# A 3x3 convolution on group-normalised images: some images by four result columns at a time, F(4,3), in pairs, the others plainly

## The chip, the cores and the metric

The kernel runs on one core of a Trainium2 chip. A core has TensorE (PE), which multiplies a 128x128 block of weights with a stream of columns into PSUM; VectorE (DVE), ScalarE (ACT) and GpSimd (POOL), which work on 128 partitions element by element; and DMA queues, of which SyncE (SP) and GpSimd issue those used here. The metric is the device time of one execution in microseconds (us), the median of several runs.

## The reference

The input holds 160 images of 128 channels and 32x32 points in float32. Each image is normalised over groups of four channels, without learned scale. The weights are five sets of 128x128x3x3 numbers, quantised in two steps from their common range. Image `i` of each five is convolved (3x3, padding 1) with set `i`, and the input is added to the result.

```python
    beta = jnp.max(U); alpha = jnp.min(U)
    s1 = (beta - alpha) / 3.0
    v1 = s1 * floor(U / s1)
    s2 = s1 / 5.0
    v2 = s2 * floor((U - v1) / s2)
    w = (v1 + v2).reshape(128 * 5, 128, 3, 3)
    act = conv(gn(x).reshape(32, 5 * 128, 32, 32), w, padding=1, groups=5)
    return x + act.reshape(x.shape)
```

## The kernel before, in words

Channels lie on the 128 partitions, and an image is a row of 1,024 float32 numbers per partition. The kernel handles the images of set 0 first, then set 1, and so on, so that "image 0 to 159" below is that order; two images make a chunk, which is loaded by one DMA. The instructions are written in the order in which each engine runs them (a manual schedule), so an engine's program order is the order of the Python calls.

Precision: a normalised image is split into a high part and a low part, both float16, and both are multiplied with the float16 integer weights.

One image goes through these steps:

- **Statistics** (`measure`, L241 and L248): two passes of ScalarE, over the sum and over the squares, far ahead of use. Means and variances of the channel groups come from small matmuls (`means`, `variances`), and small operations of VectorE, ScalarE and GpSimd make the reciprocal deviation from them (`deviations_by_vector`, `deviation`, `power`, `scales_by_vector`).
- **Combinations.** From image 7 on there are two kinds. A *combined* image uses F(2,3) across columns: for each pair of neighbouring result columns, four combinations of four input columns replace six products by four. `outer_columns` (L678) and one subtraction (L708) on GpSimd and `combine` (L690, L697) on VectorE make a float32 tile `v` of 2,048 columns; `high_combined` (ScalarE, L738) takes its high part and `low_combined` (VectorE, L744) its low part. A *row* image is normalised on GpSimd (L714), its high part (L648) is used as it stands, and only its low part (L751) is combined, over pairs of rows (`combinations`, L764 to L773). `combined()` says which kind an image is: every second up to 30, then three of five, and from image 130 three of four.
- **Products** (`product` L843, `taps` L788): a combined image takes 24 matmuls (four combinations, three rows of taps, two parts) of 512 or 496 columns, a row image 18 for the high part and 12 for the low part. The two middle combinations go to the banks `m1` and `m2_ps` one image ahead (`sums_of_pairs`). ScalarE takes `m2_ps` out (`leave`, L891), VectorE writes half the sum and half the difference into the two result banks (`pairs`, L903 and L905), and the other products add to them.
- **Result.** ScalarE copies the banks to SBUF (L929), and a DMA of GpSimd's queue adds them in DRAM to the image, which SP's queue had stored there before (L953, `store_input` L968). The first three and the last four images are added by VectorE instead (L946, L936).

The weights of the next set are quantised meanwhile on VectorE and ScalarE in small steps (`Later`, `make_column`), put between the other operations. GpSimd's operations on images are tied by `after` to an operation of VectorE, so that they run beside `pairs`. Images are loaded again into a buffer (of eleven) when its images have been combined or normalised.

Of the kernel before, what the change touches and what calls it, by code (L numbers as in the profile page):

```python
# [8 lines left out]
F32 = mybir.dt.float32  # L9
I32 = mybir.dt.int32  # L10
MM = mybir.dt.float16
# [11 lines left out]
LAST = 4  # L23
# [3 lines left out]
LIFT = 2.0**14  # L27
# [3 lines left out]
WIDEST = 40.0  # L31
# [5 lines left out]
class Later:  # L37


    def __init__(self, steps=(), pace=0.0):  # L40
        self.steps = iter(steps)
        self.pace, self.due = pace, 0.0
        self.scalar = False

    def next_image(self):
        self.due += self.pace

    def take(self, count, last=None):
        for _ in range(count):
            if not self.scalar and self.due >= 1.0:  # L50
                step = next(self.steps, None)
                self.scalar = step is SCALAR
                if not self.scalar:
                    last = step or last
                    self.due -= 1.0
        return last

    def take_scalar(self):
        if self.scalar:
            next(self.steps)  # L60
            self.scalar = False

    def finish(self):
        run(self.steps)
# [141 lines left out]
class Statistics:  # L206
# [5 lines left out]
    def __init__(self, nc, small, gavg, mhalf, nb, scale, name):  # L212
        self.nc, self.small, self.gavg, self.mhalf = nc, small, gavg, mhalf
        self.nb, self.scale, self.name = nb, scale, name
        self.late = self.shifted = False
# [74 lines left out]
    def deviations_by_vector(self):  # L290
# [3 lines left out]
        self.ngm, self.twice, self.dv = (self.tile(tag, [self.nb]) for tag in ("ngm", "twice", "dv"))  # L294
        means = self.pg[:, 0, :]
        vector.tensor_scalar_mul(self.twice, means, 2.0)
# [7 lines left out]
    def scales_by_vector(self):  # L304

        vector = self.nc.vector
        vector.tensor_scalar_mul(self.rstd, self.rstd, self.scale)
        if self.shifted:
            self.shift = self.tile("shift", [self.nb])
            vector.tensor_tensor(self.shift, self.ngm, self.rstd, ALU.mult)  # L310

    def scales(self):
# [5 lines left out]
        self.twice = self.tile("twice", [self.nb])  # L318
        nc.gpsimd.tensor_scalar_mul(self.twice, self.ngm, 2.0)
# [66 lines left out]
class Main:  # L386
# [24 lines left out]
    STAT_LEAD = 15  # L411
    FURTHER = 11
    LOAD_LEAD = 18
    CHUNKS = 11
    STEADY = 7
    BY_VECTOR = (8, 10, 11, 14, 19, 24, 29, 34)
    FIFTHS = 30
    THIRDS = 130
    EARLY = 8
    FIRST = 3  # L420
    HURRIED = (0, 2, 4, 8, 24)
# [6 lines left out]
    def __init__(self, tc, ctx, keep, x, u, out):  # L428
# [20 lines left out]
        self.rows = pool("rows", 5)  # L449
        self.wide = pool("wide", 2)  # L450
        self.wide_parts = pool("wide_parts", 4)
        self.evac = pool("evac", 2)
        self.sums = pool("sums", 3)
        self.unread = pool("unread", 1)
        self.small = pool("small", 3)
        self.ps_eo = pool("ps_eo", 2, space=PSUM)
# [8 lines left out]
        self.pair = [self.m1a, self.m2_ps]  # L465

# [4 lines left out]
        self.tables, self.wts, self.across = {}, {}, {}  # L471
        self.columns = []

        cuts = [0, 2, 4, 8, 12, 16, 20, *range(24, self.imgs + 1, 8)]
# [88 lines left out]
    def keep_taps(self, n, col):  # L563

        P = self.P
        if n not in self.tables:
            self.tables[n] = self.wpool.tile([P, ROW, 5, P], MM, tag="wt", name=f"wt{n}")
# [9 lines left out]
    def sums_across(self, n, engine):  # L577

        across = self.across[n] = self.wpool.tile(
            [self.P, 2, ROW, self.P], MM, tag="across", name=f"across{n}"  # L580
        )
        yield from self.both_sums(
            engine, across[:, 0], across[:, 1], *(self.tables[n][:, c, self.G] for c in range(ROW))
        )

    def sums_of_set(self, n):

        wt = self.tables[n]
        yield from self.both_sums(
            self.nc.vector, wt[:, :, self.SUM], wt[:, :, self.DIFF],  # L590
            *(wt[:, :, k] for k in range(ROW)),
        )
        yield from self.sums_across(n, self.nc.vector)
# [15 lines left out]
    def stats_of(self, k):  # L609
        if k not in self.stats:  # L610
# [5 lines left out]
            self.stats[k].shifted = not self.combined(self.groups[k].start)  # L616
# [699 lines left out]
```

## Time and profile before

| what | value |
|---|---|
| median of 3 runs | 967.3 us (965.7 to 967.39) |
| the profiled execution, its own time | 964.56 us |
| its span on the core | 962.5 us |
| TensorE busy | 927.8 us |
| VectorE busy | 902.6 us |
| ScalarE busy | 862.7 us |
| GpSimd busy | 460.1 us |
| moved by DMA | 254.22 MB, mean 264 GB/s |
| granted TensorE clock, mean | 0.995 |

The busy time of an engine is the union of its instructions' spans. Neighbouring instructions of VectorE and of ScalarE overlap by some hundredths of a microsecond, and matmuls by more, so a row's mean time for one is longer than the distance at which they follow each other. A row of the table of groups reads: line, engine, operation, output <- inputs, shapes, count | busy us, mean ns of one | idle us of the engine just before, and what ended it.

### The profile page before, as it was taken

What the parts mean: (1) busy time and instruction counts of PE and PEld (TensorE: products, weight loads), DVE (VectorE), ACT (ScalarE), POOL (GpSimd) and SP (SyncE); (2) the same over time, 40 slices, a digit from 0 to 9 for tenths busy, and PEclk for the clock granted to TensorE, in tenths of its full rate; (3) what the DMA queues carried; (4) which work ended last, traced back from release to release, by engine and by line L of the source; (5) the groups of instructions that cost most, each with busy time, mean ns of one, the idle gap of its engine ahead of it and who ended that gap; (6) DMA issues with size and microseconds to landing.
All of it is one profiled execution on the core that took longest, in us unless ns stands there. A gap on an engine that the chain in (4) does not pass through costs nothing.

```text
span 962.5 us, 13034 instructions
## 1 busy us (share of the span) xinstructions
PE 927.8 (96%) x4432; PEld 433.8 (45%) x4432; DVE 902.6 (94%) x1269; ACT 862.7 (90%) x1167; POOL 460.1 (48%) x477
## 2 busy tenths in 40 slices
PE   2899989999999999999999999999999999999997
PEld 1344434444444444444444444444444444444443
DVE  7989999999899999989999999899999998999993
ACT  5879989999899999999999999999999999997660
POOL 4344434456445445554545445545444366565640
PEclk9999999999999999999999999999999999999999
DMA  9079999999999999999999999999999999856563
GB/s 349 36 267 345 334 348 320 325 321 325 328 321 323 317 295 308 272 306 254 295 251 289 284 293 297 282 277 286 267 273 267 282 279 269 172 91 107 91 107 112
DMA packets 67450, 254.22 MB, mean 264 GB/s; under 512 B 5296, under 2 KB 5296, under 8 KB 67376
## 3 DMA queue, kind: packets, MB, share of 16 engines
q1 hardware_dynamic: 45344, 173.09, 48.0%
q0 software_dynamic: 22032, 80.23, 44.4%
q8 instruction: 36, 0.59, 0.2%
q14 instruction: 38, 0.31, 0.1%
HBM read 89.19 MB, written 164.10 MB: 263 GB/s over the span
## 4 chain that ended last, share of the span: by engine, by line


## 5 line engine op out<-in xcount | busy, mean ns | idle before, releaser
L788 PE MATMUL eo<-hi,wt 128*128 128x496 f16 (+3 forms) x1170 | 310.8, 376 | 2.4 <-DVE eo L905 1.7
L843 PEld LDWEIGHTS <-wt 128*128 128x128 f16 x1884 | 183.9, 99 | 211.5 <-DVE eo L905 2.7
L744 DVE SCALAR_TENSOR_TENSOR vl<-v,rstd,vh 128x2048 f16<-128x2048 f32 x94 | 221.8, 2360 | 0.2 <-ACT vh L738 0.2
L843 PE MATMUL eo<-vh,wt 128*128 128x512 f16 x561 | 210.1, 375 | 1.2 <-DVE eo L905 1.2
L843 PE MATMUL eo<-vl,wt 128*128 128x512 f16 x561 | 210.1, 374 | 0.0
L738 ACT ACTIVATE vh<-v,rstd 128x2048 f16<-128x2048 f32 x94 | 188.2, 2002 | 4.8 <-DVE v L697 4.3
L929 ACT COPY sum<-eo 128x1024 f32<-128x1024 f32 x153 | 161.0, 1052 | 32.3 <-PE eo L843 31.7
L788 PEld LDWEIGHTS <-wt 128*128 128x128 f16 x1242 | 121.2, 99 | 142.8 <-DVE eo L905 4.9
L678 POOL TENSOR_SCALAR v<-xt,ngm 128x64 f32<-128x64 f32 x94 | 79.1, 842 | 202.0 <-DVE vl L744 86.9
L248 ACT ACTIVATE junk<-xt,mv 128x1024 uint8<-128x1024 f32 x152 | 174.4, 1148 | 0.3
L241 ACT ACTIVATE junk<-xt 128x1024 uint8<-128x1024 f32 x152 | 160.5, 1056 | 13.3 <-DMA xt<-in_x_dram 10.0
L714 POOL TENSOR_SCALAR z<-xt,ngm,rstd 128x1024 f32<-128x1024 f32 x49 | 93.3, 1904 | 165.1 <-DVE rows L773 55.0
L843 PEld LDWEIGHTS <-across 128*128 128x128 f16 x1128 | 110.8, 98 | 131.9 <-issue 4.9
L843 PE MATMUL eo<-rows,wt 128*128 128x512 f16 x378 | 143.5, 380 | 0.0
L953 POOL DMA_DIRECT2D out_dram<-sum x153 | 133.7, 874 | 14.4 <-ACT sum L929 6.6
L690 DVE TENSOR_TENSOR v<-xt 128x960 f32<-128x960 f32 x94 | 114.0, 1212 | 0.0
L843 PE MATMUL m<-vl,across 128*128 128x496 f16 (+1 forms) x282 | 106.4, 377 | 2.1 <-DVE vl L744 2.1
L891 ACT ACTIVATE m<-m 128x512 f32<-128x512 f32 x157 | 93.7, 597 | 14.1 <-PE m L843 13.7
L843 PE MATMUL m<-vh,across 128*128 128x496 f16 (+1 forms) x282 | 106.2, 376 | 0.2 <-ACT m L891 0.2
L708 POOL TENSOR_TENSOR v<-xt 128x512 f32<-128x512 f32 x94 | 97.2, 1034 | 0.0
L751 DVE TENSOR_TENSOR lo<-z,hi 128x1024 f16<-128x1024 f32 x66 | 80.6, 1221 | 0.0
L286 POOL TENSOR_TENSOR rstd<-ve,mhalf 128x8 f32<-128x8 f32 (+2 forms) x24 | 42.3, 1761 | 65.1 <-DVE rows L773 21.1
(150 smaller groups left out, 1166.3 us busy)
## 6 DMA issues: line engine op xcount, KB each, us to landing
xt<-in_x_dram SPq DMA_DIRECT2D x78, 1024.0 KB, 9.6
out_dram<-sum POOLq DMA_DIRECT2D x153, 512.0 KB, 8.7
out_dram<-xt SPq DMA_DIRECT2D x76, 1024.0 KB, 14.2
out_dram<-xt SPq DMA_DIRECT2D x7, 512.0 KB, 3.3
u<-in_L_conv_U_dram SPq DMA_DIRECT2D x4, 576.0 KB, 13.6
xt<-in_x_dram SPq DMA_DIRECT2D x4, 512.0 KB, 10.1
range<-in_L_conv_U_dram SPq DMA_DIRECT2D x3, 576.0 KB, 8.3
u<-in_L_conv_U_dram SPq DMA_DIRECT2D x2, 288.0 KB, 3.1
```

The lines of the kernel that those rows point to most:

```text
L241: self.nc.scalar.activation(junk, image, ACTF.Copy, scale=-1.0 / image.shape[1], accum_out=self.mv[:, j, 0:1],)
L248: self.nc.scalar.activation(junk, image, ACTF.Square, bias=self.mv[:, j, 0:1], accum_out=self.mv[:, j, 1:2],)
L690: nc.vector.tensor_tensor(self.view(v, 1, (511, 2), (half, H), (1, half - 1)), self.view(x, 1, (1, 2), (W, H), (2, half - 1)), self.view(x ...
L708: ins = nc.gpsimd.tensor_sub(self.v[i][:, 1536:], odd, even)
L714: ins = nc.gpsimd.tensor_scalar(z, self.image(i), st.ngm[:, j], st.rstd[:, j], ALU.add, ALU.mult)
L738: self.nc.scalar.mul(vh, self.v[i], st.rstd[:, j])
L744: yield self.nc.vector.scalar_tensor_tensor(vl, self.v[i], st.rstd[:, j], self.hi[i], ALU.mult, ALU.subtract)
L788: nc.tensor.matmul(self.bank(target, a)[:, first:end, c0:c1], self.wts[n, col][:, k, :], tile[:, s0 : s0 + 2 * (end - first) - 1 : 2, c0 + ...
L843: self.nc.tensor.matmul(out, weights, moving, start=start and j == 0, stop=False, skip_group_check=True)
L891: self.nc.scalar.mul(m2, self.m2_ps, 0.5)
L929: nc.scalar.copy(self.as_banks(i, self.sum[i]), self.flat(i, eo))
L953: added = self.nc.gpsimd.dma_start(self.ov[n, :, b], self.sum.pop(i), accum_op=ALU.add)
```

## The change

Two kinds of images remain after image 4. **Quad** chunks (43 of the 80, list `QUADS`; 86 images) use F(4,3) across columns: four neighbouring result columns come from six combinations of six input columns, for both images of the chunk at once. The other 69 images are **plain**: both parts go through all nine taps as they stand, 36 matmuls of up to 512 columns. A quad image takes 36 matmuls of 256 or 248 columns (six combinations, three rows of taps, two parts).

- On GpSimd, `differences` makes the difference of the left and right neighbours of every point (960 points by one subtraction, and the two edge columns by two operations of 32 points each). `combine`'s share of GpSimd and the normalising there are gone.
- On VectorE, `inner_points` and `outer_points` make the six combinations of a chunk from the image and from the differences. They read every fourth number of a row (`every_fourth`, a step of 16 bytes). `low_quad` takes the low part (1,536 columns per image), `high_quad` on ScalarE the high part. `combinations`, `pairs` and the row kind are gone but for images 3 and 4.
- The four inner products of an image go to `m1` and `m2_ps`, two to a bank. `leave` takes `m2_ps` out; `sum_and_difference` (four operations on PSUM for a chunk) and `four_points` (four on SBUF) make the four result columns' share. Two columns are started in the result banks, where the two outer products are added (`quad_main`), and two are written to every fourth place of `quad_sum`; `quad_result` copies the other two beside them, and one DMA adds both images in DRAM.
- Plain images are normalised and split on ScalarE, their low part is made on VectorE (1,024 columns), and their banks are copied out by ScalarE as before.
- The loop runs over **units**: one quad chunk with one plain image (23 units) or two (20 units), after nine single images and before the last two, which are plain. `unit` writes each engine's order: TensorE does the inner products of the chunk, the first plain image, the outer products and, if there is one, the second plain image.
- Statistics are made in groups of five images rather than eight, eight image buffers replace eleven, the tables of a set hold five combinations of the three columns of taps, and four images rather than eight are measured on VectorE.

```diff
-    BY_VECTOR = (8, 10, 11, 14, 19, 24, 29, 34)
+    CHUNKS = 8
+    BY_VECTOR = (8, 10, 11, 14)
+    QUADS = (5, 7, 9, 11, 13, *(c for c in range(15, 64) if c * 7 % 12 < 7), *(c for c in range(64, 79) if c % 3))
...
+    def differences(self, i):
...
+        return [
+            pool.tensor_scalar(d[:, :, 0:1], x[:, :, 1:2], st.ngm[:, k], 1.0, ALU.add, ALU.mult),
+            pool.tensor_scalar(
+                d[:, :, W - 1 :], x[:, :, W - 2 : W - 1], st.ngm[:, k], -1.0, ALU.add, ALU.mult
+            ),
+            pool.tensor_sub(d[:, :, 1 : W - 1], x[:, :, 2:], x[:, :, : W - 2]),
+        ]
+    def every_fourth(self, t, start, count=1):
+        return self.view(t, start, *([(1, count)] if count > 1 else []), (4, 512))
+    def inner_points(self, c):
+        u = self.u[c] = self.wide.tile([self.P, 6, NB, 256], F32, tag="u", name=f"wide{c}")
+        vector = self.nc.vector
+        x = self.chunks[c]
+        ab = u[:, 3:6:2].rearrange("p k j q -> p k (j q)")
+        vector.scalar_tensor_tensor(
+            ab, self.every_fourth(x, 0, 2), -4.0, self.every_fourth(x, 2, 2), ALU.mult, ALU.add
+        )
+        for j in range(NB):
+            st, k = self.column_of(c * NB + j)
+            vector.scalar_tensor_tensor(
+                u[:, 2, j], u[:, 5, j], st.six[:, k], u[:, 3, j], ALU.add, ALU.add
+            )
+        vector.tensor_sub(u[:, 4], u[:, 5], u[:, 3])
+    def outer_points(self, c):
+        u, d, vector = self.u[c], self.d.pop(c), self.nc.vector
+        flat = u.rearrange("p k j q -> p k (j q)")
+        vector.scalar_tensor_tensor(
+            flat[:, 0:2], self.every_fourth(d, 2, 2), 0.25, self.every_fourth(d, 0, 2),
+            ALU.mult, ALU.subtract,
+        )
+        for slot, by in ((3, 2.0), (5, -2.0)):
+            vector.scalar_tensor_tensor(
+                flat[:, slot], self.every_fourth(d, 1), by, self.every_fourth(d, 2),
+                ALU.mult, ALU.add,
+            )
...
+    def quad_product(self, target, i, slot, start):
+        n, _ = self.place(i)
+        eighth = self.W // 4
+        for step in self.KS:
+            shift = (step - 1) * eighth
+            first, end = max(0, -shift), 256 - max(0, shift)
+            for j, source in enumerate((self.hi[i], self.v[i])):
+                self.nc.tensor.matmul(
+                    target[:, first:end],
+                    self.quads[n][:, slot - 1, step] if slot else self.wts[n, 0][:, step],
+                    source[:, slot, first + shift : end + shift],
...
+    def sum_and_difference(self, i):
...
+        for k, op in enumerate((ALU.add, ALU.subtract)):
+            self.nc.vector.scalar_tensor_tensor(
+                self.sd[c][:, k, :, j], m13, THIRDS, m24, ALU.mult, op
+            )
+    def four_points(self, c):
...
+        vector.tensor_add(flat[:, 0], sd[:, 0, 0], sd[:, 0, 1])
+        vector.scalar_tensor_tensor(flat[:, 1], sd[:, 1, 1], 8.0, sd[:, 1, 0], ALU.mult, ALU.add)
+        for k, by, s in ((1, 2.0, 1), (2, 4.0, 0)):
+            vector.scalar_tensor_tensor(
+                self.every_fourth(total, k), sd[:, s, 1], by, sd[:, s, 0], ALU.mult, ALU.add
+            )
...
+    def unit(self, u):
...
+        for j in range(NB):
+            if coming is not None:
+                self.high_quad(coming * NB + j)
+            for which in (1, 0):
+                self.sum_of_pairs(c * NB + j, which)
+            self.leave(c * NB + j)
+        self.left_over()
+        take(1)
+        for j in range(NB):
+            if wide is not None:
+                before = self.last_but_one()
+                for ins in self.differences(wide * NB + j):
+                    self.after(ins, before)
+            self.sum_and_difference(c * NB + j)
...
+        if mine:
+            self.main(mine[0], 0, first_place)
...
+        self.four_points(c)
...
+                self.low_quad(coming * NB + j)
...
+            self.main(mine[0], 1)
...
+        self.quad_main(c, second_place)
...
+            self.inner_points(wide)
...
+            self.outer_points(wide)
...
+            self.low_part(prepared[0])
+        if len(mine) > 1:
+            self.quad_result(c)
...
+            self.main(mine[1], 0, self.columns_on_the_way)
...
+            self.main(mine[1], 1)
```

## The prediction

> **What bounds the kernel now.** First I read the busy table and the stretches. The lines give the length of the stretch, then for each engine its busy time, then TensorE's granted clock, the DMA engines' share and GB/s.
>
> ```profile
> PE 927.8 (96%) x4432; PEld 433.8 (45%) x4432; DVE 902.6 (94%) x1269; ACT 862.7 (90%) x1167; POOL 460.1 (48%) x477
> ...
> 0.00:60.00 60.00, 38.13 (x176) 18.11 (x177) 51.09 (x101) 38.56 (x62) 24.24 (x52) 0.97 0.49 183
> 300.00:500.00 200.00, 199.53 (x958) 93.39 (x957) 191.53 (x265) 193.08 (x264) 97.98 (x95) 1.00 1.01 290
> 830.00:940.00 110.00, 110.00 (x526) 51.33 (x525) 102.24 (x117) 84.66 (x98) 64.73 (x56) 1.00 0.63 100
> ```
>
> From 150 us to 940 TensorE never rests; DVE is at 96% beside it and ACT at 97%. So work must leave two or three engines to shorten anything. The chain that ended last is empty in this profile, so I go by busy time and waits: the waits show TensorE waiting some 2 us in all for any one row after the start, and GpSimd waiting for DVE all the time (87 us at L678 for L744 alone).
>
> Next, how close matmuls follow each other (timeline of TensorE):
>
> ```profile
> 119.39 0.33 PE L558 MATMUL small<-ident,m 128*128 128x128 f16 x3
> 119.55 0.80 PE L788 MATMUL eo<-hi,wt 128*128 128x496 f16 x3
> ```
>
> Three of 496 columns end 0.80 after the first began, and one lasts 0.38: one per 0.21 us. Three of 128 columns: (0.33-0.22)/2 = 0.056, each with its own weight load. So a weight load hides under even 128 columns.
>
> Then VectorE's rows, by shape:
>
> ```profile
> L744 DVE SCALAR_TENSOR_TENSOR vl<-v,rstd,vh 128x2048 f16<-128x2048 f32 x94 | 221.8, 2360 | 0.2 <-ACT vh L738 0.2
> L697 DVE SCALAR_TENSOR_TENSOR v<-xt,twice 128x512 f32<-128x512 f32 x94 | 69.9, 744 | 0.0
> L903 DVE SCALAR_TENSOR_TENSOR eo<-m1b,m 128x512 f32<-128x512 f32 x79 | 54.7, 692 | 16.4 <-PE m1b L843 11.9 <-ACT m L891 4.5
> L142 DVE SCALAR_TENSOR_TENSOR tt<-nnn,s1nhi,u 128x384 f32<-128x384 int16 x13 | 9.6, 739 | 0.0
> L142 DVE SCALAR_TENSOR_TENSOR tt<-nnn,s2nhi,rest 128x384 f32<-128x384 int16 x15 | 9.2, 613 | 0.1
> ```
>
> An element costs (2.36-0.744)/1536 = 1.05 ns. The two last rows are one operation; the first reads `u` in steps of 12 bytes, the second `rest` without gaps: 0.126 us more for 384 elements, 0.33 ns each. L690 and L697 read in steps of 8 bytes and pay nothing (744 fits the same line as 613).
>
> Last, two instructions from GpSimd's and VectorE's timelines:
>
> ```profile
> 488.22 1.03 POOL L708 TENSOR_TENSOR v<-xt 128x512 f32<-128x512 f32 x1
> 488.29 1.99 DVE L690 TENSOR_TENSOR v<-xt 128x960 f32<-128x960 f32 x1
> ```
>
> L690 takes 1.15 elsewhere. Begun 0.07 after GpSimd's, it took 0.84 more: the whole rest of that operation. The other way round, GpSimd's L714 lasts 3.2 us where it begins under a low part. So the two exclude each other, and `pairs`, which reads PSUM, is where GpSimd runs freely.
>
> **What the Trainium skill says.** TensorE: Matmul & The Clock Gate, Back-to-back issue gap: columns over 2.4 GHz plus 2.5 ns; the trace's 0.056 and 0.21 agree. SBUF — State Buffer, Who interferes with whom: a VectorE instruction with two SBUF inputs and a GpSimd instruction that reads SBUF exclude each other for a whole instruction; the pair above agrees. Advanced Engine Details and Errata, SBUF Cachelines: lines of 16 bytes, and at least two hits on a line are needed to absorb the latency. The 12-byte row agrees in kind; 16-byte steps hit every line once, and no row of this trace has them.
>
> **The change, part by part.** I cost the stretch from the first unit to the last, and what lies around it.
>
> *TensorE.* Quad image: 12 matmuls of 256 columns at 0.109 and 24 of 248 at 0.106 (between 0.056 and 0.21): 3.85 us, 7.7 a chunk. Plain image: 36 at 0.208: 7.5. Before: 24x0.21 = 5.1 combined, 30x0.21 = 6.3 row. 43 chunks and the 63 plain images of the units: 331+472 = 803 us; 5.38 an image, against 5.68 that an image took between 250 and 590 us.
>
> *VectorE, one chunk.* `sum_and_difference` 4x0.69 = 2.8; `four_points` 0.68+3x0.744 = 2.9; `low_quad` 2x1.82 = 3.6; `inner_points` 1.28+2x0.48+0.68 = 2.9; `outer_points` 1.28+2x0.744 = 2.8. That is 15.0; 17 instructions overlap by 0.08 each, as successive starts in the timeline show: 13.6. Beside it: 65 low parts at 1.14 = 74; 24 groups of statistics at 0.95 = 23; four sets of weights at 21 (some 40 operations of 0.35 to 0.74 less the overlap) = 84. Sum 43x13.6+74+23+84 = 766. The work per image is what it was before (about 5.25 for a combined image, 3.75 for a row one): `pairs` and the row kind go, six combinations come.
>
> *Two costs that no row shows whole.* (a) `inner_points` and `outer_points` read 3,072 elements a chunk in 16-byte steps. From 0 at 8 bytes through 0.33 ns at 12, a straight line gives 0.68 at 16: 2.1 us a chunk. Ends: 0, and a doubled cycle, 3.2; with `four_points`' 1,024 strided writes also doubled 4.3. For the writes I take 0, having no row. (b) GpSimd's `differences`: 960 points at 1.03/512 are 1.93, the edges under 0.37 each: 5.3 us a chunk of reading. Free of two-input VectorE work is `sum_and_difference` alone, 2.7; 2.6 remain to exclude VectorE. Ends: 0 (VectorE waits anyway) and 2.6; I take 2.0. Behind the blocked instruction stand `four_points` and `low_quad`, for which TensorE's outer products and the next chunk's inner ones wait; that is how this reaches TensorE.
> VectorE's stretch: 766+43x(2.1+2.0) = 942, over TensorE's 803. It sets the pace.
>
> *ScalarE.* Chunk: two high parts 3.0, two `leave` 1.0, result 0.95; plain: 1.13+0.94+0.95 = 3.0; measuring 2.2 an image; weights about 20. 212+190+320+20 = 742: below both. If its strided result doubled, 39 more, still below.
>
> *GpSimd and DMA.* 112 adding DMAs at 0.87 for 153. Bytes are the same; 254 MB at the 344 GB/s seen between 60 and 150 us are 740 us, hidden under VectorE. Eight image buffers rather than eleven make loads later: SP's queue already waits 300 us for L697 to free buffers, and the stores queued behind it gain no reader; I take 0 for it. If that cover is gone, ScalarE's measuring waits, as 10.0 us did at the start.
>
> *Around it.* Image 4 is done at 74.6 us and stays; images 5 to 8 plain at 7.5: first unit at 105. After the last unit two plain images, 15.0, and 6.7 from the last matmul to the end. Sum: 105+942+21.7 = 1,069 of span. The profiled execution's own time is 2.1 over its span and the median 2.7 over that: **1,074 us**.
>
> **The rivals.** *TensorE stays the bound (faster).* If (a) and (b) together cost less than 1.6 us a chunk, VectorE needs under 835 and the time falls below 967. At nothing, TensorE's 803 decide: 105+803+21.7+4.8 = 935. Units with one plain image (15.2 on TensorE, about 17 on VectorE) push it towards 960. For it: single-input strided L134 loses only 0.05. Against it: the 12-byte row and the pair above, both measured here.
> *Only one of (a) and (b) is there:* 766+43x2.05 = 854, so 986; with some waits of TensorE up to 1,030. For it: VectorE's waits can give GpSimd its window, and reads in both inputs may overlap.
> *Both at their ends:* 43x6.9 = 297; 105+766+297+21.7+4.8 = 1,195.
> *The small matmuls don't hide their weight loads:* 98 ns on 3,096 of them, 300 us. The 0.056 speaks against it; under 1 in 50, within the last case.
>
> **How the numbers follow.** The likeliest case 0.5 (its own range 1,030 to 1,165); one cost alone 0.24 (985 to 1,030); TensorE-bound 0.16 (935 to 962); the upper ends 0.08; no difference 0.02. Differences under 0.2% can't be told from none here. The range 950 to 1,165 leaves out the best of the fast case and the upper ends. Faster 0.16, same 0.02, slower 0.82.
>
> **What would show it.** Right: VectorE at 97% or more in the units and TensorE at some 80%; the 1,024-element reads of `inner_points` near 2.0 us rather than 1.28; `four_points` or the low part before it stretched by 1 to 2 us beside GpSimd's subtraction; TensorE waiting for `eo` or `vl`. Wrong: those reads at 1.28, no stretched rows, or TensorE at 99%; a first unit well off 105 us; ScalarE waiting for loads.

## The result, and the profile after

The changed kernel takes **1,192.9 us** (median of 4 runs, 1,192.1 to 1,193.2), the one before 966.7 in the same comparison: 1.234 times as long, 95% interval 1.232 to 1.236. The forecast was slower, at 1,074, with a range up to 1,165; the time lies 119 us above the forecast and outside the range. The span of the profiled execution is 1,190.9 us, where the forecast had 1,069.

The busy table on the page of the changed kernel:

```profile
PE 982.7 (83%) x5966; PEld 611.0 (51%) x5966; DVE 993.0 (83%) x1320; ACT 877.2 (74%) x1138; POOL 424.2 (36%) x449
```

And a stretch of the units, in the columns used before (busy PE, PEld, DVE, ACT, POOL, then the clock, the DMA engines' share and GB/s):

```profile
300.00:500.00 200.00, 175.19 (x1071) 109.52 (x1072) 167.78 (x220) 156.03 (x199) 74.09 (x74) 0.92 0.81 229
```

No engine is full any more. The kernel before had TensorE at 100% and VectorE at 96% in such a stretch. Now they are at 88 and 84%, and TensorE's clock is below full speed too. Every engine waits for another one, so the next view is the waits (engine, waiting line, what ended the wait: us in total, how often, longest):

```profile
PE m L861 <- ACT m L912: 127.8, 25, 10.9
...
ACT vh L747 <- DVE wide L714: 80.5, 22, 7.1
...
DVE sd L935 <- PE m1b L861: 46.9, 15, 8.2
DVE sd L935 <- PE m1a L861: 45.5, 25, 4.0
...
PE small L250 <- ACT junk L235: 40.9, 12, 6.0
```

Read together, these are a ring. TensorE's inner products (L861 into `m`) wait for ScalarE's `leave` (L912). `leave`, the copy of the bank `m2_ps` to SBUF, stands in ScalarE's order behind `high_quad` (L747) of the coming chunk. That waits for VectorE's outer points (L714; in 27.4 us more, for L301 right after them). And VectorE's `sum_and_difference` (L935) waits for TensorE's inner products. One turn of the ring is in the timeline of all engines (start, us, engine, line, operation; in brackets the idle time before and what ended it):

```profile
511.14 0.27 PE L861 MATMUL m1b<-vl,quads 128*128 128x248 f16 x1
511.72 2.09 DVE L714 SCALAR_TENSOR_TENSOR wide<-d 128x512 f32<-128x512 f32 x2
511.77 0.80 ACT L128 ACTIVATE nnn<-u,s1r 128x384 int16<-128x384 f32 x1
...
514.05 1.57 ACT L747 ACTIVATE vh<-wide,rstd 128x1536 f16<-128x1536 f32 x1 [1.48 <-DVE rstd L301]
...
515.53 0.58 ACT L912 ACTIVATE m<-m 128x512 f32<-128x512 f32 x1
...
516.16 0.37 PE L861 MATMUL m<-vh,quads 128*128 128x256 f16 x1 [4.75 <-ACT m L912]
516.33 0.42 PE L861 MATMUL m<-vl,quads 128*128 128x256 f16 x1
516.39 1.78 POOL L681 TENSOR_TENSOR d<-xt 128x960 f32<-128x960 f32 x1
...
517.35 1.91 DVE L767 TENSOR_TENSOR lo<-z,hi 128x1024 f16<-128x1024 f32 x1
...
519.32 0.27 PE L861 MATMUL m1a<-vh,quads 128*128 128x248 f16 x1
...
520.45 1.29 DVE L935 SCALAR_TENSOR_TENSOR sd<-m1a,m 128x512 f32<-128x512 f32 x2 [1.19 <-PE m1a L861]
```

TensorE stops at 511.4 and starts at 516.16. `leave` itself takes 0.58 us and its input was complete at 510.1 (the last of those matmuls, begun at 509.86); ScalarE was free for it at 512.57, after a step of the weights (L128), so some 3 us of its delay come from the 1.57 us high part ahead of it, which had waited for VectorE. And then TensorE is slow: matmuls of 256 and 248 columns follow each other at 0.17 to 0.22 us until 519.2, and at 0.10 to 0.11 afterwards. VectorE, which had stood idle for only 0.21 us until then, waits 1.19 us for them. The Trainium skill (TensorE: Matmul & The Clock Gate, What's actually happening) says that an idle window of some 3.4 us halves TensorE's clock until a busy one has passed. This trace agrees: about half speed for some 3 us after a wait of 4.75. In the 42 units counted below, each of the 29 waits of 3.1 us or more was followed by slow matmuls for 2.8 to 6.5 us, and none of the 8 waits up to 1.25 us was. The lines of GpSimd and VectorE show the exclusion that the forecast costed: the low part (L767) lasts 1.91 us beside the subtraction, 1.29 in the mean.

Last, the groups by shape that answer to the disputed costs (count | busy us, mean ns of one | idle before):

```profile
L695 DVE SCALAR_TENSOR_TENSOR wide<-xt 128x1024 f32<-128x1024 f32 x43 | 87.3, 2030 | 0.7
L953 DVE SCALAR_TENSOR_TENSOR quad_sum<-sd 128x512 f32<-128x512 f32 x86 | 86.7, 1091 | 0.0
L950 DVE TENSOR_TENSOR eo<-sd 128x512 f32<-128x512 f32 x43 | 42.1, 979 | 0.0
L963 ACT COPY quad_sum<-eo 128x1024 f32<-128x1024 f32 x43 | 86.0, 2000 | 13.1 <-PE eo L861 13.1
```

The strided reads (L695; L709 and L714 are alike, at 2,001 ns and 1,068) cost a little more than the forecast took. The strided writes (L953, L963), taken at nothing, cost about as much per element (e11 below). L950, an addition in `four_points`, is longer by 0.3 us in the mean, but that mean mixes two cases: 27 of its 43 executions last at most 0.77 us, and 16, which meet GpSimd's subtraction, last 1.04 to 1.66, up to 0.97 longer.

**Where the 122 us of span come from.** The inner products of the first unit start at 114.4 us (forecast 105). Image 4 was done in time, but the averaging matmul of a group of statistics (L250) stood ahead of image 5's products and waited for VectorE's measuring (L229):

```profile
83.05 0.56 PE L250 MATMUL small<-mv,gavg 128*128 128x4 f32 x2 [8.59 <-DVE mv L229]
```

The last unit ends some 23 us before the end (forecast 21.7). The units between take 1,053.5 us, where the forecast had 942. In them VectorE is busy for 893 us, less than forecast, and idle for 161 us, which the forecast had at nothing.

TensorE's side of it can be added up. From the first `sum_and_difference` of the first unit to that of the last (42 units, 1,030 us) I take the starts of successive matmuls. Gaps over 0.3 us are waits; the excess over the full-clock distance (0.107 us for 256 columns, 0.216 for 512), where it is more than a quarter, is slow clock; the rest is work. This gives **801 us of work, 169 us of waits and 61 us of slow clock**; the border between the first and the last moves by some 5 us with the distance that is taken for short matmuls. The waits are the two rows of TensorE above: 127.8 for `leave`, 40.9 where the small matmul of `means` (L250), placed between the two images' outer products, waits for ScalarE's measuring.

### The profile page after: what moved, and what is told of

Read it like the earlier page. It is cut to its first block, busy times and chain, and to the rows that moved or that the text cites. A ratio compares the mean times of both kernels' runs of the same rounds, so it can differ in the third digit from the quotient of the medians.

```text
span 1190.9 us, 15714 instructions
## 1 busy us (share of the span) xinstructions
PE 982.7 (83%) x5966; PEld 611.0 (51%) x5966; DVE 993.0 (83%) x1320; ACT 877.2 (74%) x1138; POOL 424.2 (36%) x449
## 4 chain that ended last, share of the span: by engine, by line
PE 44%; DVE 37%; ACT 12%; issue 5%; POOL 1%; DMA 0%; DVEq 0%; ACTq 0%; POOLq 0%
PE eo L804 24%; PE m L861 9%; DVE vl L755 7%; PE m1a L861 5%; DVE wide L714 4%; DVE wide L709 4%; DVE wide L695 4%; DVE quad_sum L953 4%; PE eo L861 3%; ACT vh L747 3%; ACT junk L235 3%; ACT junk L242 2%; DVE eo L950 2%; DVE sd L935 2%; PE m1b L861 2%
## 5 line engine op out<-in xcount | busy, mean ns | idle before, releaser
L861 PEld LDWEIGHTS <-quads 128*128 128x128 f16 x2580 | 274.6, 106 | 182.0 <-issue 132.6
L804 PE MATMUL eo<-hi,wt 128*128 128x496 f16 (+1 forms) x1314 | 354.7, 381 | 2.5 <-ACT sum L995 1.0
L804 PE MATMUL eo<-lo,wt 128*128 128x496 f16 (+2 forms) x1278 | 341.7, 378 | 0.0
L861 PE MATMUL m<-vh,quads 128*128 128x256 f16 x516 | 139.7, 306 | 128.0 <-ACT m L912 127.8
L747 ACT ACTIVATE vh<-wide,rstd 128x1536 f16<-128x1536 f32 x86 | 134.8, 1568 | 112.5 <-DVE wide L714 80.5
L235 ACT ACTIVATE junk<-xt 128x1024 uint8<-128x1024 f32 x156 | 164.7, 1056 | 13.5 <-DMA xt<-in_x_dram 11.3
L681 POOL TENSOR_TENSOR d<-xt 128x960 f32<-128x960 f32 x86 | 154.0, 1791 | 0.0
L755 DVE SCALAR_TENSOR_TENSOR vl<-wide,rstd,vh 128x1536 f16<-128x1536 f32 x86 | 153.6, 1808 | 0.0
L861 PE MATMUL m<-vl,quads 128*128 128x256 f16 x516 | 140.4, 308 | 0.0
L767 DVE TENSOR_TENSOR lo<-z,hi 128x1024 f16<-128x1024 f32 x74 | 95.4, 1289 | 17.7 <-ACT hi L646 17.7
L935 DVE SCALAR_TENSOR_TENSOR sd<-m1a,m 128x512 f32<-128x512 f32 x86 | 55.4, 685 | 65.5 <-PE m1a L861 45.5
L935 DVE SCALAR_TENSOR_TENSOR sd<-m1b,m 128x512 f32<-128x512 f32 x86 | 55.3, 685 | 60.4 <-PE m1b L861 46.9
L995 ACT COPY sum<-eo 128x1024 f32<-128x1024 f32 x69 | 69.6, 1009 | 43.8 <-PE eo L804 41.9
L963 ACT COPY quad_sum<-eo 128x1024 f32<-128x1024 f32 x43 | 86.0, 2000 | 13.1 <-PE eo L861 13.1
L912 ACT ACTIVATE m<-m 128x512 f32<-128x512 f32 x88 | 51.9, 590 | 59.0 <-PE m L861 58.5
L638 ACT ACTIVATE z<-xt,shift,rstd 128x1024 f32<-128x1024 f32 x74 | 91.7, 1240 | 3.1 <-POOL shift L310 3.1
L709 DVE SCALAR_TENSOR_TENSOR wide<-d 128x1024 f32<-128x1024 f32 x43 | 86.0, 2001 | 4.5 <-POOL d L681 4.5
L714 DVE SCALAR_TENSOR_TENSOR wide<-d 128x512 f32<-128x512 f32 x86 | 88.0, 1068 | 0.0
```

The lines of the kernel that those rows point to most:

```text
L235: self.nc.scalar.activation(junk, image, ACTF.Copy, scale=-1.0 / image.shape[1], accum_out=self.mv[:, j, 0:1],)
L638: nc.scalar.activation(z, self.image(i), ACTF.Identity, bias=st.shift[:, j : j + 1], scale=st.rstd[:, j : j + 1],)
L681: pool.tensor_sub(d[:, :, 1 : W - 1], x[:, :, 2:], x[:, :, : W - 2]),
L709: vector.scalar_tensor_tensor(flat[:, 0:2], self.every_fourth(d, 2, 2), 0.25, self.every_fourth(d, 0, 2), ALU.mult, ALU.subtract,)
L714: vector.scalar_tensor_tensor(flat[:, slot], self.every_fourth(d, 1), by, self.every_fourth(d, 2), ALU.mult, ALU.add,)
L747: self.nc.scalar.mul(vh, self.u[c][:, :, j], st.rstd[:, k])
```

## The experiments

All were compared with runs of the kernel before on the same chip (966.3 to 966.8 us). For each I give, beside the time, the account just described, and the mean period of a unit from one first `sum_and_difference` to the next, by kind: one plain image among the first 33 units (in which weights are still made), one plain image in the last nine, two plain images. Account and periods are those of the profiled execution, which lies within 3.5 us of the median, in e7 5.8 us above it. In e8 to e10, 35 units have two plain images; the first and the last two have one, and are left out.

| run | us | ratio, 95% interval | TensorE: work + waits + slow clock | one plain, early / late | two plain |
|---|---|---|---|---|---|
| changed kernel | 1,192.9 | 1.232 to 1.236 | 801 + 169 + 61 | 23.5 / 21.6 | 26.6 |
| e1 leave first | 1,180.1 | 1.218 to 1.223 | 803 + 158 + 57 | 23.1 / 19.9 | 27.1 |
| e2 dense reads | 1,127.3 | 1.164 to 1.168 | 801 + 119 + 48 | 21.0 / 18.7 | 26.6 |
| e3 no GpSimd read | 1,187.9 | 1.228 to 1.232 | 801 + 163 + 65 | 23.5 / 21.8 | 26.5 |
| e4 = e1 and e2 | 1,142.8 | 1.180 to 1.189 | 802 + 132 + 45 | 21.4 / 18.1 | 27.2 |
| e5 means late | 1,165.4 | 1.204 to 1.208 | 799 + 152 + 54 | 23.5 / 21.6 | 25.3 |
| e6 both late | 1,175.4 | 1.211 to 1.218 | 802 + 151 + 60 | 23.9 / 19.8 | 26.4 |
| e7 = e6 and e2 | 1,129.8 | 1.166 to 1.170 | 802 + 119 + 55 | 22.3 / 18.2 | 26.3 |
| e8 even units | 1,099.8 | 1.135 to 1.139 | 847 + 72 + 27 | none | 25.8 |
| e9 = e8 and e5 | 1,068.9 | 1.104 to 1.108 | 844 + 51 + 16 | none | 24.8 |
| e10 = e9 and e2 | 1,035.1 | 1.070 to 1.074 | 844 + 29 + 10 | none | 24.1 |
| e11 dense writes | 1,176.6 | 1.215 to 1.219 | 801 + 154 + 62 | 23.1 / 21.1 | 26.6 |
| e12 half measuring | 1,179.3 | 1.218 to 1.223 | 800 + 156 + 61 | 23.4 / 21.5 | 26.1 |

TensorE's work is the same to 0.5% in all kernels with 43 chunks. What the edits move are its waits and, with them, its clock.

**First question: order on ScalarE, or VectorE's work?** Theory H said that `leave` behind `high_quad` is the cause; theory V, that VectorE's added work (strided reads, exclusion) is. Four runs: the order changed, the reads made dense, GpSimd's read taken away, and the first two together.

The first, e1:

```diff
         for j in range(NB):
-            if coming is not None:
-                self.high_quad(coming * NB + j)
             for which in (1, 0):
                 self.sum_of_pairs(c * NB + j, which)
             self.leave(c * NB + j)
+        for j in range(NB):
+            if coming is not None:
+                self.high_quad(coming * NB + j)
```

> All work is kept; on ScalarE the copies out of m2_ps (leave) of both images now stand ahead of the two high parts of the coming chunk. Theory H (handover): leave, which only needs TensorE, stands behind a high part that waits for the last operations of VectorE's previous unit, so that TensorE waits for the bank, its clock falls, and VectorE waits for TensorE. Then the wait of TensorE for leave (128 us) goes to under 20 us, VectorE's busy share in the units rises from 86% to 93% or more, and the time falls by 70 to 120 us, to 1,075 to 1,120. Theory V (VectorE's work alone sets the pace, as predicted): its operations are the same, so 1,185 to 1,200.

The second, e2, in `inner_points` and `outer_points` alike:

```diff
-            ab, self.every_fourth(x, 0, 2), -4.0, self.every_fourth(x, 2, 2), ALU.mult, ALU.add
+            ab, self.dense(x, 0, 2), -4.0, self.dense(x, 2, 2), ALU.mult, ALU.add
```

> The combinations read 512 neighbouring numbers instead of every fourth (as many elements, other data; the result is not the convolution). Both theories: the reads of 1,024 elements last 1.28 us instead of 2.0 and those of 512 0.74 instead of 1.07, 2.1 us a chunk, 91 us in all. Theory V: the time falls by 85 to 95 us, to about 1,100. Theory H: these operations stand in the loop from VectorE over ScalarE and TensorE back to VectorE, so the time falls by at least 91, and more where TensorE's clock stays up: 1,060 to 1,100.

The third, e3:

```diff
-            pool.tensor_sub(d[:, :, 1 : W - 1], x[:, :, 2:], x[:, :, : W - 2]),
+            pool.memset(d[:, :, 1 : W - 1], 0.5),
```

> GpSimd fills the 960 points of the differences with a constant instead of subtracting (it then reads only the edge columns; the result is not the convolution). If the exclusion of GpSimd's reads and VectorE's two-input operations costs what the prediction took (2.0 us a chunk) the time falls by 86 us. From the stretched rows of the changed kernel (L950 0.98 instead of 0.69, L767 1.29 instead of 1.22, L703 0.76 instead of 0.68) it is 26 us at most: 1,165 to 1,190.

The fourth has the edits of e1 and e2 together.

> The first two edits together (the result is not the convolution). Theory H: 975 to 1,030, since VectorE's 885 us of work in the units less 91 is about TensorE's 803, and units with one plain image leave TensorE some waits. Theory V: as the second edit alone, about 1,100.

Of the four, only e3 fell in a range set for it; e1, e2 and e4 miss the ranges of both theories.

The waits of e1:

```profile
ACT m L912 <- PE m L861: 150.8, 66, 5.6
...
PE small L250 <- ACT junk L235: 69.1, 14, 8.6
...
PE m L861 <- ACT m L912: 44.2, 15, 12.6
```

TensorE's wait for `leave` fell from 128 to 44 us, so the order was what put some 84 us of it there. But only 12.8 us came off the time. ScalarE now stands at the head of its queue and waits for TensorE (150.8 us, 58.5 before the edit), and is late for other things instead: the averaging matmul waits 69 us rather than 41, and the matmuls of plain images wait 35 us for a low part, which they had not done before. H as a whole falls: the bank was the place of the wait, and only in small part the cause of the lost time.

A row of e2, answering to L695:

```profile
L699 DVE SCALAR_TENSOR_TENSOR wide<-xt 128x1024 f32<-128x1024 f32 x43 | 52.5, 1221 | 0.7
```

Against 2,030 ns: 0.79 ns for each element of the result, both of whose inputs are read at a step of 16 bytes. The Trainium skill (Advanced Engine Details and Errata, SBUF Cachelines) says that an access pattern that hits each 16-byte line once pays; these rows agree. VectorE lost 102 us of busy time in the 42 units (885 to 783) and the kernel 66. They came off unevenly: 2.5 to 2.9 us for a unit with one plain image, nothing for one with two. So VectorE's work counts in one kind of unit alone, and V falls as a full explanation too. e4 is slower than e2. In it ScalarE's `leave` waits 152 us for TensorE's products, against 63 in e2; I take this for the reason, but no run isolates it.

A row of e3, the exclusion taken away:

```profile
L950 DVE TENSOR_TENSOR eo<-sd 128x512 f32<-128x512 f32 x43 | 29.6, 689 | 0.0
```

The lock is real (979 ns fall to 689, and the low part's 1,289 to 1,222), as the Trainium skill has it (SBUF — State Buffer, Who interferes with whom), but small: 25 us of VectorE's time, 0.6 us a chunk where the forecast took 2.0. Without it the time is only 5 us less. GpSimd still reads the edge columns in e3, so a remainder of the exclusion is not in this figure.

**Second question: ScalarE's place in the order, or its amount? And the units' unevenness?** Theory Q said that TensorE's order of issue meets ScalarE at two bad places; S, that ScalarE is late as such; U, that units with one and with two plain images load the engines so differently that one unit's slack doesn't serve the next.

e5 moves the averaging matmul:

```diff
-            self.columns_on_the_way()
...
-        self.quad_main(c, second_place)
+        self.quad_main(c, self.columns_on_the_way)
+        if len(mine) < 2:
+            second_place()
...
             self.main(mine[1], 1)
+            second_place()
```

> Edit: the small matmul that averages the groups' sums no longer stands between the two images' outer products, where it waited for ScalarE's measuring (12 waits, 40.9 us); it is issued after the second plain image's matmuls, or after the outer products where a unit has one plain image. Theory Q (TensorE's order of issue puts it behind ScalarE at two places, and each wait also halves its clock for some microseconds): these 41 us of gaps and some 25 us of half clock go, but the wait for the bank that `leave` empties stays at 120 us or takes part of it over: 1,140 to 1,175. Theory S (ScalarE as a whole is late; where TensorE meets it doesn't matter): the wait reappears at the bank: 1,180 to 1,195.

e6 has the edits of e5 and e1, and this one:

```diff
-            for which in (1, 0):
+            for which in ((1, 0), (0, 1))[j]:
```

> Edit: both places at once. ScalarE empties the bank of the inner products before it makes the coming unit's high parts, the second image's products for the other bank go first, and the averaging matmul is issued late. Theory Q: TensorE's waits for ScalarE fall from 169 us to under 70, its half clock from 192 us to under 90, and the time to 1,060 to 1,120; the units with one plain image stay near 22 us each because of VectorE's strided reads. Theory S: the waits go on elsewhere (the results' banks, the plain images' parts), 130 us or more, and the time is 1,165 to 1,185.

e7 has those of e6 and e2.

> Edit: as the run with both places changed, and VectorE's reads of the inner and outer points are contiguous (the images' columns are then no longer taken by fours, so this leaves the computation of the convolution; every operation keeps its count and size). Without the order's change, dense reads gave 1,127. Theory Q: with both obstacles gone, the first-to-last stretch is 850 to 910 us against TensorE's 803 of work, and the time 990 to 1,050. Theory S: 1,110 to 1,145, no better than dense reads alone.

e8 changes the list of chunks:

```diff
-    QUADS = (5, 7, 9, 11, 13, *(c for c in range(15, 64) if c * 7 % 12 < 7), *(c for c in range(64, 79) if c % 3))
+    QUADS = (*range(5, 79, 2), 78)
```

> Edit: every unit has one pair of images in fours and two plain images (38 pairs rather than 43), instead of units with one and with two plain images mixed. TensorE's work is then 38x7.7+73x7.5 = 840 us in the units, VectorE's with its strided costs about 860. Theory U (the time is lost because uneven units load the engines unevenly: VectorE decides in those with one plain image, TensorE in those with two, and the shared banks don't let one unit's slack serve the next): each unit takes some 23 us, and the time is 1,010 to 1,050. Theory Q (the waits lie inside each unit with two plain images, 26.6 us each now): 38 units at 26 to 27 us, 1,115 to 1,170.

e5 moves one small matmul and gains 27.5 us: the averaging's 41 us of waits are gone, the bank's rose from 128 to 143. All of the gain is in the units with two plain images (26.6 to 25.3), where most of the wait was. That lies in Q's range. The wait for the bank in e5:

```profile
PE m L861 <- ACT m L912: 142.7, 31, 10.9
```

e6, with both places changed, is slower than e5. Its groups of matmuls (idle before, and what ended it):

```profile
L804 PE MATMUL eo<-hi,wt 128*128 128x496 f16 (+1 forms) x1314 | 370.1, 394 | 34.8 <-ACT sum L995 33.4 <-ACT wt L570 0.7 <-DVE eo L923 0.7
L804 PE MATMUL eo<-lo,wt 128*128 128x496 f16 (+2 forms) x1278 | 360.4, 394 | 50.3 <-DVE lo L767 50.3
```

Waits that were 1.0 and nothing in the changed kernel (result banks not copied out, low parts not made) are now 33 and 50 us. So Q's promise that both places can be opened is not kept, and the time lies in S's range, 1,165 to 1,185. `leave` first makes ScalarE wait for TensorE (171 us), and what ScalarE does next comes late. It is a ring, and moving `leave` moves the wait along it. e7 says the same with dense reads: no gain over e2, in S's range again.

e8 gives 93 us at once, although the account has 46 us more work of TensorE with 38 chunks for 43 (what follows the last unit's first `sum_and_difference` is 8 us shorter in return). Its waits for the bank are 18.5 us (9) rather than 127.8 (25). It lies between U's range and Q's, and the averaging still waits:

```profile
PE small L250 <- ACT junk L235: 43.9, 16, 6.0
...
PE m L861 <- ACT m L912: 18.5, 9, 9.2
```

A unit in which nothing stops TensorE takes 23.1 us, which is its work at full clock. The units with two plain images in which the averaging waits take 27.8 in the mean, the others 24.4. e8 changes two things, though: the units are even, and there are five chunks fewer, which takes work from VectorE (busy for 885 us in the units of the changed kernel, for 827 in e8). The runs don't separate these two.

**Third question: what is left.**

e9 has the edits of e8 and e5, e10 those of e8, e5 and e2.

> Edit: two changes together: every unit has one pair in fours and two plain images (1,099.8 us alone), and the averaging matmul is issued after the second plain image (1,165.4 us alone). In the run with even units TensorE took 23.1 us a unit where nothing stopped it and 28.5 where the averaging matmul waited for ScalarE (16 waits, 43.9 us, each followed by half clock). If TensorE is now the engine that decides, these waits and some 25 to 40 us of half clock go: 1,020 to 1,050. If ScalarE is too late as such, TensorE meets it at the banks instead: 1,080 to 1,100.

> Edit: as the run before it, with contiguous reads for the inner and outer points (leaves the computation of the convolution). It takes 2.1 us of VectorE's work out of each of 38 units, 80 us. If TensorE decides with even units, VectorE's strided reads are hidden and the time falls by less than 20 us. If VectorE decides, it falls by 50 to 80.

e11, the writes:

```diff
-                self.every_fourth(total, k), sd[:, s, 1], by, sd[:, s, 0], ALU.mult, ALU.add
+                self.view(total, (k - 1) * 512, (1, 512)), sd[:, s, 1], by, sd[:, s, 0], ALU.mult, ALU.add
...
-            self.view(total, 0, (3, 2), (4, 512)), eo.rearrange("p k h w -> p k (h w)")
+            self.view(total, 1024, (512, 2), (1, 512)), eo.rearrange("p k h w -> p k (h w)")
```

> Edit to the changed kernel as it is: only the writes of the results are contiguous (VectorE's two columns, 0.35 us shorter each, 30 us in all; ScalarE's two, 0.95 us, 41 us in all); the columns of the result then stand in the wrong places, so this leaves the computation of the output's order. The forecast took both at nothing. If they are paid as the reads are (66 of 91 us), the time is 1,165 to 1,175; if they lie in the engines' idle time, 1,185 to 1,193; if ScalarE's lateness alone makes the waits, below 1,155.

e12, the measuring passes:

```diff
-            junk, image, ACTF.Copy, scale=-1.0 / image.shape[1],
+            junk[:, :512], image[:, :512], ACTF.Copy, scale=-2.0 / image.shape[1],
...
-            junk, image, ACTF.Square, bias=self.mv[:, j, 0:1],
+            junk[:, :512], image[:, :512], ACTF.Square, bias=self.mv[:, j, 0:1],
```

> Edit to the changed kernel as it is: ScalarE's two measuring passes read half of each image (leaves half of the statistics' computation). This takes some 0.45 us from about 300 passes, 130 us of ScalarE's work, and moves nothing. Theory S (the sum of ScalarE's work is too large for it to be on time): both of TensorE's waits for it go, 1,060 to 1,110. Theory Q (ScalarE's emptying of the bank stands behind a high part that waits for VectorE's outer points, so no speed of ScalarE's helps there): only the averaging matmul's waits go, some 40 us with their half clock up to 65; the bank's stay at 110 us or more; 1,130 to 1,165.

e9 is at 1,068.9, 124 us under the changed kernel and the shortest of those that leave nothing out, yet 10.6% above the kernel before. It lies between its two expectations: the averaging's waits are gone, and those for the bank rose from 18.5 to 31.5 us; nearly all the rest of its 51 us is TensorE's transposing of new weights (L558), which waits 19.2 us for VectorE. e10 took 90 us of VectorE's busy time from the 37 units counted there (830 to 740) and gained 34, again between the two. The period of a unit fell from 24.8 to 24.1, where 23.1 is TensorE's own: with even units VectorE's work still costs something in some of them, TensorE's decides in most.

e11:

```profile
L953 DVE SCALAR_TENSOR_TENSOR quad_sum<-sd 128x512 f32<-128x512 f32 x86 | 55.3, 684 | 0.0
L963 ACT COPY quad_sum<-eo 128x1024 f32<-128x1024 f32 x43 | 43.1, 1003 | 12.7 <-PE eo L861 12.7
```

The rows fell from 1,091 ns and 2,000. That is 0.8 us a chunk of VectorE's time, 35 in all, and 1.0 of ScalarE's, 43 in all; the time fell by 16.2, to just above the first of its three ranges. The forecast's zero for the writes was wrong by that much.

e12 is the clearest of the runs. Its waits:

```profile
PE m L861 <- ACT m L912: 128.1, 25, 10.0
...
ACT vh L747 <- DVE wide L714: 104.2, 24, 8.0
...
PE small L250 <- ACT junk L235: 25.3, 12, 3.6
```

ScalarE lost 116 us of busy time in the units (785 to 669), and TensorE waits for `leave` as before, 25 times and 128 us. ScalarE only stands idle longer ahead of its high part (104 us rather than 80). The time fell by 13.6, nearly what the averaging's wait lost (40.9 to 25.3). The gain is below Q's 1,130 to 1,165, since that wait was shortened, not removed; but S, with 1,060 to 1,110, is out, though e6 and e7 had come as it said. The amount of ScalarE's work is not what makes `leave` late; in the averaging's wait, which is for the measuring itself, it has a part.

**What the runs settle.** The account of the changed kernel, by kind of unit (us a unit):

| kind (units) | period | TensorE: work + waits + slow clock | VectorE busy |
|---|---|---|---|
| one plain, early (14) | 23.5 | 15.6 + 6.9 + 1.0 | 21.1 |
| one plain, late (9) | 21.6 | 15.6 + 4.2 + 1.9 | 17.3 |
| two plain (19) | 26.6 | 23.3 + 1.8 + 1.6 | 22.8 |

The two waits belong to different kinds. Of the 127.8 us before the bank, 126 lie in units with one plain image, 91 of them in the early ones. There TensorE has 5.5 us less work than VectorE is busy, so most of that wait is slack that TensorE must spend somewhere, and opening the bank moves it. It fits e1, which took 84 us off the wait and 13 off the time. Of the averaging's 41 us, 32 lie in units with two plain images, where TensorE has the most work; moving it took 25 us off these units (e5).

Units with one plain image take 23.5 us (VectorE is busy for 21.1 of them, TensorE for 16.6); their period follows VectorE's work and little else that was tried (21.0 with dense reads, 23.4 with less measuring). In the last nine such units no engine is busy for more than 17.5 of 21.6 us; they shorten with dense reads and with `leave` first, as a ring of dependent steps would, but no run took the ring apart. Units with two plain images take 26.6 us (TensorE 24.8 busy, 22.7 in the shortest unit); they don't shorten with VectorE's work, but do with the place of the averaging. Even where a wait is slack, TensorE pays for it in the clock afterwards: the slow matmuls after a bank's wait fall in the next unit, as in the turn of the ring shown.

How much of e8's gain is due to evenness, and whether a place for `leave` exists that holds up neither TensorE nor ScalarE, stays open; no such place was found in the four runs that moved it (e1, e4, e6, e7). A second buffer for the wide points or another bank, which would loosen the ring, was not tried.

**A bound on the change itself.** If TensorE never waited in the units of the changed kernel, the span would be 117.3 (first `sum_and_difference`) + 801 + 43.3 (from the last unit's to the end) = 962 us, an estimate from this account. That is the span of the kernel before, 962.5. By this estimate the change could not have gained measurably on TensorE with this start and this list of chunks. With VectorE's 885 us of busy time in place of the 801, the same sum gives 1,046.

## Why the prediction was right or wrong

The direction was right; the size was not. VectorE's strided reads were foreseen and cost about what was said, but the largest part of the miss is idle time that the forecast had at nothing. Step by step:

- **TensorE's pitch and sum: right.** Matmuls of 256 columns follow at 0.107 us, weight loads hidden, and the account gives 801 us for 42 units. With the last one it is some 824, where the forecast had 803 for all 43: the small matmuls (transposes of weights, averages), left out, are some 10 of these 21 us.
- **(a), strided reads, 2.1 us a chunk: right in kind, nearly in size.** 102 us of busy time over 42 chunks are 2.4 each. The straight line from 8 over 12 to 16 bytes served; it gives 0.66 ns at 16, where the forecast wrote 0.68 and the rows show 0.75 to 0.79.
- **(a), strided writes taken at nothing: wrong.** 0.8 us a chunk on VectorE and 1.0 on ScalarE; together they cost 16 us of time (e11). The forecast had no row for them and chose the lower end.
- **(b), exclusion by GpSimd, 2.0 us a chunk: wrong in size.** 0.6 a chunk, 5 us of time (e3). GpSimd's subtraction begins beside `sum_and_difference`, where VectorE reads PSUM or waits for TensorE; in the turn of the ring shown it stretched one low part. Where the two meet, the stretch is as long as forecast (L950 by up to 0.97 us), but in 16 of the 43 chunks only.
- **VectorE's bare work, 766 us: near.** 893 us busy in the units less 102 for the reads, 28 for the writes (885 to 857 in e11) and 25 for the exclusion leave 738.
- **"VectorE's stretch: 766+43x(2.1+2.0) = 942 [...] It sets the pace": this is the step that failed.** VectorE's work was over-estimated by 49 us, and its idle time, taken as none, was 161. A sum over all units sets the pace only if the engine with the largest sum is never stopped. Here VectorE stands idle in every kind: in the 42 units counted, 34 us in the early ones with one plain image, 39 in the late ones and 73 in those with two, where TensorE's own 23.3 us are above VectorE's 22.8 before any wait. That the banks `m1` and `m2_ps` and the one buffer of the wide points tie the engines to each other within a unit is read from the order of the waits; no run took one of these ties away.
- **ScalarE, "742: below both": right as a sum and wrong as a use.** It was busy for 794 us in the units; the forecast's own clause on the strided result (39 more) covers most of the difference. But I costed ScalarE by its sum alone, and its place in the order not at all. TensorE waited for it 169 us, and the slow clock added 61. That the averaging matmul stands ahead of the second image's outer products is shown to matter: moving it gave 27.5 us (e5). That `leave` stands behind a high part explains where TensorE waits, and little of the time (e1). Both places could be read in `unit` before the run. e12 shows that ScalarE's sum had no part in the bank's wait.
- **First unit at 105 us: 9 us too early.** TensorE's 8.6 us wait for VectorE's measuring, shown above, and some 3 us of slow clock after it are of this size; the forecast had no wait there. Loads did not become the limit, as taken: ScalarE's measuring waits 11.3 us for them in all, against 10.0 before.
- **The rivals.** "TensorE stays the bound" did not come; by the bound above it would have been about 964, not 935. "Only one of (a) and (b)" describes the costs best, but its 986 "with some waits of TensorE up to 1,030" allows 44 us of waits where waits and slow clock came to 230. "Both at their ends" gave 1,195, within 3 us of the result, by luck: the runs show the costs in the middle of their ranges or below it, and the time went into waits.
- **What would show it.** The reads near 2.0 us came. "VectorE at 97% or more in the units" did not (893 of 1,053.5, 85%), and this is what told at first sight that the sum was not the bound. "TensorE at some 80%" came out at 84%, but with 61 us of slow clock in it.

## What to carry to other kernels

When an edit leaves two or three engines with nearly equal sums, the largest sum is a lower bound and no forecast: take one period of the loop, write down each engine's order in it, and follow who waits for whom around the ring, kind of period by kind. Look for a short instruction that stands in its engine's order ahead of work that is ready, and waits for another engine: moving the averaging matmul gave 27.5 us. Before removing a wait, ask whether the waiting engine has slack in that kind of period: taking 84 us off the bank's wait gave 13. And price a wait of TensorE of more than some 3 us at more than its length, since it runs slowly afterwards.

## What the hardware showed that I had not expected

- Writing at a step of 16 bytes costs VectorE as much per element as reading both inputs so: 1,091 ns against 684 for 512 float32 elements written (0.79 ns each), and 2,030 against 1,221 for 1,024 elements whose two inputs are read so (0.79). ScalarE pays more: 2,000 ns against 1,003 for 1,024 written from PSUM (0.97 ns each).
- TensorE's slow clock is a notable part of a loss by waits: 61 us beside 169 in the changed kernel, 16 beside 51 in e9. Its mean granted clock fell from 0.995 to 0.920, and is higher again where the waits are fewer: 0.973 in e9, 0.983 in e10. In the changed kernel's units every wait of 3.1 us or more brought slow matmuls, and no wait up to 1.25 us did.
- The exclusion between GpSimd and VectorE, which stretched 16 of 43 executions of one addition by 0.35 to 0.97 us, cost 25 us of VectorE's 885 although GpSimd read SBUF for 154 us in that subtraction.
